# A third buffer of one-hots for an eighth slot of gathered rows, in a graph attention kernel

## The chip, the cores and the metric

The kernel runs on one core of a Trainium2 chip. Its time is the device time of that core in microseconds (us), and the number to watch is the median of several runs. The core has a matrix engine (TensorE, PE in a profile), a vector engine (VectorE, DVE), a scalar engine (ScalarE, ACT), GpSimd (POOL) and SyncE (SP), each with an instruction stream of its own that is worked off in order, and 16 DMA engines that move data between main memory and the core's own memory.

## The reference

One layer of attention on a graph, with 12,500 nodes of 128 features and 212,500 edges that are sorted by their target node (`dst`). Each edge has 128 features of its own. The computation, cut to what matters:

```
Q, K, V = x @ WQ, x @ WK, x @ WV          # per node, 8 heads of 16
Eh      = edge_attr @ WE                  # per edge
score   = exp(clip(sum_per_head(K[src] * Q[dst] / 4 * Eh), -5, 5))
wV, Z   = segment_sum(V[src] * score, dst), segment_sum(score, dst)
h       = x + wV / (Z + 1e-6)
y       = batch_norm(h) * gamma + beta    # mean and variance over all nodes
out     = layer_norm(x + y)               # over the 128 features
```

K and V of the source node are needed for every edge: these rows are fetched by an index. Q of the target node and the sums over the target node are handled with one-hot matrices, because the edges are sorted by target.

## The kernel before, in words

The edges are cut into 1661 tiles of 128. A group has up to 8 tiles in two halves of 4, and there are 208 groups. There are three stages.

**The node table** (loop over `q`, 25 steps). TensorE multiplies the transposed node features by the weights of K and V, VectorE and ScalarE copy the result out of PSUM in turn (L263, L262), and SP stores it as the table `kvd` in main memory (L605). The table is whole only at the end of this stage, so rows of it can be gathered only then. The first 8 groups (0 to 7) do without it. For their edges GpSimd gathers rows of x itself (`slot<-x`), and K and V are made from those: TensorE transposes them (L278, `turn_x`) and multiplies them by the weights (L285, `project`). Some of these groups, `EARLY` of them, are projected during the table's stage at steps spread by `piece` (L614 to L616), and their K and V go into a slot of gathered rows. The others are projected in the main loop one group ahead (`project_main`, L423, called at L681), into other buffers named `t`.

**The main loop** over the groups `g` (L671). The order of all instructions is written by hand: each engine gets its instructions in the order in which these lines call for them. For group g, VectorE multiplies the gathered K by Q times the edge features (`products`, L520), sums per head (L527), clips (L532), and multiplies the gathered V by the exponentials (`message`, L539). Between these it works for other groups; the one that matters here is `onehot(g + 1)`, right behind the message of g, which compares the target numbers of a tile with a row of 0 to 127 (L451 to L454) and so makes the matrix that sums edges into nodes. TensorE uses it one iteration later in `gather_sum` (L554). The one-hots lie in a tile named `oh`.

**The last stage** normalises over the nodes and writes the output. It needs x again, which SP loads into slots that have become free (`load_x`, L407) after the last group has been given one.

**The slots.** `NSLOT` tiles `slot0`, `slot1`, ... of 8 KiB in each partition hold gathered rows. One slot takes two groups of gathered x rows, or one group of K and V rows. A slot becomes free when the message of its group is made (L544), or, for a pair of x groups, when the second of them is projected (L288). Each time `load_kv` (L234) gives the free slot to the next group and queues eight gathers. In the main loop it issues at once all but seven of what is queued. The rest are issued one by one behind steps of VectorE, each with a wait on that step (`pace`, L206), in the order in which the groups come. All gathers are on GpSimd, which works them off in order, so one whose slot is not yet free holds up those behind it. In twelve of the later groups the eighth tile of rows comes by single-row loads on SP instead (`fetch_rows`, L225), into tiles named `byrow`.

Of the kernel before, what the change touches and what calls it, by code (L numbers as in the profile page):

```python
# [8 lines left out]
F32 = mybir.dt.float32  # L9
# [7 lines left out]
P = 128  # L17
# [4 lines left out]
U = 4  # L22
WN = 64
CH = 512
NSLOT = 8
NX = 8
EARLY = 4
RUN = 64
ROWS = 8
FIRST_ROW = 5  # L30
# [32 lines left out]
def gnn_kernel(  # L63
# [35 lines left out]
    wp = lps.enter_context(tc.tile_pool(name="work", bufs=2))  # L99
# [83 lines left out]
    KV, XG, SLOT, PAIR = {}, {}, {}, {}  # L183
    free = list(range(NSLOT))
    pending = list(range(nxg, NG))
# [3 lines left out]
    def slot(i):  # L189
        return rows.tile([P, 2 * G * P], F32, name=f"slot{i}")  # L190
# [15 lines left out]
    def pace(step):  # L206
        if queued:
            f, *a = queued.pop(0)
            tc.add_manual_dep(f(*a).ins, step.ins.name,
                              mybir.DependencyInfo(mybir.DependencyClass.Sync, mybir.DependencyReason.DATA),  # L210
                              reason="pace")
# [34 lines left out]
    for g in range(nxg):  # L246
        if g % 2 == 0:
            PAIR[g // 2] = free.pop(0)
            t = slot(PAIR[g // 2])
# [161 lines left out]
    def nt(g):  # L411
        return sizes[g]
# [29 lines left out]
    def onehot(g):  # L442


        n, m = usizes[2 * g], usizes[2 * g + 1]
        t = wp.tile([P, U * P + U * WN], F32, name="oh", bufs=2)
        one = t[:, :n * P].rearrange("p (a b) -> p a b", b=P)
        two = t[:, U * P:U * P + m * WN].rearrange("p (a b) -> p a b", b=WN)
        OH[g] = [one[:, j, :] for j in range(n)] + [two[:, j, :] for j in range(m)]
        r = rel[:, starts[g]:starts[g] + nt(g)]  # L450
        nc.vector.tensor_tensor(one, iota_ps[:, None, :].to_broadcast([P, n, P]),  # L451
                                r[:, :n, None].to_broadcast([P, n, P]), op=OP.is_equal)
        nc.vector.tensor_scalar(one[:, :, WN], r[:, :n], lim[:, 2 * g:2 * g + 1], None, op0=OP.is_equal)
        pace(nc.vector.tensor_tensor(two, iota_ps[:, None, :WN].to_broadcast([P, m, WN]),  # L454
                                     r[:, n:, None].to_broadcast([P, m, WN]), op=OP.is_equal))
# [156 lines left out]
    NQ = -(-NB // 4)  # L612
    early = min(EARLY, nxg)
    piece = {}  # L614
# [34 lines left out]
    load_kv()  # L649
    ehqe(1)  # L650
    onehot(0)
    within(load, 2)
    turned_onehot(2)
# [17 lines left out]
    for g in range(NG):  # L671
# [26 lines left out]
        if g == NG - 1:  # L698
# [3 lines left out]
            nc.scalar.activation(warm, eps, AF.Sqrt)  # L702
        within(message, g)
        within(onehot, g + 1)
        if g == 2:
            load_last()
# [259 lines left out]
```

## Time and profile before

| what | value |
|---|---|
| median of 3 runs | 2808.24 us (2806.66 to 2818.62) |
| the profiled execution's own time | 2148.92 us |
| its span, from first to last instruction | 2147.0 us |
| busy: TensorE, VectorE, ScalarE, GpSimd | 1681.1, 1640.5, 630.7, 1592.5 us |
| gathers of table rows on GpSimd | 1585, first at 86.2 us, last at 2076.0 us |
| gathers of x rows on GpSimd | 64, first at 3.0 us, last at 82.8 us |
| mean granted TensorE clock | 0.941 |

The profile is of one execution. The times in it are from the start of its span. "Busy" is the time in which an engine executed something. The idle time ahead of a group of instructions is put down to what released the instruction, where that can be seen, and to "issue" where nothing that the profile shows was waited for. The profiled execution is much shorter than the runs. All durations below are from the profiled execution.

### The profile page before, as it was taken

What the parts mean: (1) busy time and instruction counts of PE and PEld (TensorE: products, weight loads), DVE (VectorE), ACT (ScalarE), POOL (GpSimd) and SP (SyncE); (2) the same over time, 40 slices, a digit from 0 to 9 for tenths busy, and PEclk for the clock granted to TensorE, in tenths of its full rate; (3) what the DMA queues carried; (4) which work ended last, traced back from release to release, by engine and by line L of the source; (5) the groups of instructions that cost most, each with busy time, mean ns of one, the idle gap of its engine ahead of it and who ended that gap; (6) DMA issues with size and microseconds to landing.
All of it is one profiled execution on the core that took longest, in us unless ns stands there. A gap on an engine that the chain in (4) does not pass through costs nothing. (4 is left out here: it accounts for less than half of the span.)

```text
span 2147.0 us, 37902 instructions
## 1 busy us (share of the span) xinstructions
PE 1681.1 (78%) x9350; PEld 1094.9 (51%) x9350; DVE 1640.5 (76%) x3571; ACT 630.7 (29%) x2509; POOL 1592.5 (74%) x1681
## 2 busy tenths in 40 slices
PE   8898888877777777777777777777877777777877
PEld 7565555554444444545444545454544544445445
DVE  4669999877877777777787777777777777777766
ACT  3343333222222222232222222222222222222226
POOL 7776777777777777777777777777777777777755
PEclk9999999999999999999999998999899999999988
DMA  9866566555655555656555555555655655655754
GB/s 304 280 190 182 180 203 191 173 180 166 181 168 168 179 167 168 182 168 178 169 173 174 170 180 168 176 171 155 189 173 168 181 167 155 192 171 161 222 163 122
DMA packets 179740, 386.86 MB, mean 180 GB/s; under 512 B 41838, under 2 KB 96151, under 8 KB 179511
## 3 DMA queue, kind: packets, MB, share of 16 engines
q0 software_dynamic: 78128, 212.05, 33.4%
q1 hardware_dynamic: 98038, 169.83, 25.7%
q10 hardware_dynamic: 3345, 2.48, 0.4%
q8 instruction: 77, 1.26, 0.2%
q14 instruction: 152, 1.25, 0.2%
HBM read 364.57 MB, written 19.63 MB: 179 GB/s over the span
## 5 line engine op out<-in xcount | busy, mean ns | idle before, releaser
L199 POOL DMA_INDIRECT slot<-kvd,srcs x1585 | 1502.9, 948 | 490.4 <-issue 202.0
L554 PE MATMUL ps_a<-msg,oh 128*128 128x136 f32 (+1 forms) x3322 | 570.1, 315 | 1.5 <-DVE msg L539 1.5
L520 DVE TENSOR_TENSOR p<-slot,ps_t 128x512 f32<-128x512 f32 (+1 forms) x408 | 272.6, 677 | 356.1 <-DMA slot<-kvd,srcs 328.4
L554 PEld LDWEIGHTS ps_a<-msg,oh 128*128 128x128 f32 (+1 forms) x3322 | 463.5, 183 | 87.5 <-issue 65.3
L534 ACT ACTIVATE ps_m<-s 128x64 f32<-128x64 f32 x208 | 47.3, 227 | 1333.8 <-DVE s L532 1045.7
L490 PE MATMUL ps_e<-ea,w_e 128*128 128x512 f32 x832 | 404.8, 610 | 2.4 <-DMA ea<-eaT 2.1
L576 PE MATMUL ps_m<-ident,at 128*128 128x128 f32 x416 | 101.6, 328 | 320.2 <-DVE oh L454 313.0
L511 PE MATMUL ps_t<-ident,wt 128*128 128x128 f32 x1661 | 243.9, 283 | 92.8 <-DVE wt L503 91.6
L576 PEld LDWEIGHTS ps_m<-ident,at 128*128 128x128 f32 x416 | 66.1, 200 | 412.3 <-ACT q L480 359.5
L503 DVE TENSOR_TENSOR wt<-wt,ps_q 128x512 f32<-128x512 f32 x416 | 265.4, 679 | 1.8 <-PE ps_q L498 1.8
L511 PEld LDWEIGHTS ps_t<-ident,wt 128*128 128x128 f32 x1661 | 184.4, 142 | 135.7 <-DVE wt L503 131.7
L527 DVE TENSOR_REDUCE s<-p 128x64 f32<-128x1024 f32 x208 | 251.6, 1210 | 0.0
L539 DVE TENSOR_TENSOR msg<-slot,ps_m 128x1024 f32<-128x1024 f32 (+1 forms) x204 | 244.7, 1200 | 1.6 <-ACT hx L582 1.4
L492 ACT ACTIVATE wt<-ps_e 128x512 f32<-128x512 f32 x416 | 227.3, 584 | 14.9 <-PE ps_e L490 12.4
L490 PEld LDWEIGHTS ps_e<-ea,w_e 128*128 128x128 f32 x832 | 146.5, 196 | 107.7 <-issue 87.1
L498 PE MATMUL ps_q<-ot,q 64*128 64x512 bf16 x1248 | 171.2, 380 | 0.0
L451 DVE TENSOR_TENSOR oh<-ps_m,rel_i 128x512 f32<-128x512 f32 x208 | 141.8, 682 | 0.0
L498 PEld LDWEIGHTS <-q 64*128 64x128 bf16 x1248 | 44.1, 94 | 186.4 <-issue 161.7
L440 ACT ACTIVATE xw<-hx 128x64 f32 x416 | 84.2, 248 | 59.8 <-issue 52.0
L582 ACT ACTIVATE hx<-ps_m 128x64 f32 x416 | 91.6, 220 | 10.4 <-PE ps_m L577 3.6
L570 DVE SCALAR_TENSOR_TENSOR at<-os,keep,rz 128x128 f32<-128x128 f32 x208 | 73.2, 352 | 24.4 <-DVE rz L566 0.9
L471 PE MATMUL ps_m<-w_q,xw 128*128 128x128 f32 x416 | 88.4, 297 | 1.6 <-ACT xw L440 0.9
(111 smaller groups left out, 1555.3 us busy)
## 6 DMA issues: line engine op xcount, KB each, us to landing
ea<-eaT SPq DMA_DIRECT2D x207, 512.0 KB
rb<-relT SPq DMA_DIRECT2D x414, 64.0 KB
slot<-kvd,srcs POOLq DMA_INDIRECT x1585
byrow<-kvd SPq DMA_DIRECT2D x1536, 1.0 KB
kvd<-t SPq DMA_DIRECT2D x24, 512.0 KB
slot<-xT SPq DMA_DIRECT2D x24, 256.0 KB
out<-o SPq DMA_DIRECT2D x24, 256.0 KB
hx<-xT SPq DMA_DIRECT2D x11, 512.0 KB
```

The costliest lines, as they stand in the source:

```text
L199: return nc.gpsimd.indirect_dma_start(out=out, out_offset=None, in_=table, in_offset=bass.IndirectOffsetOnAxis(ap=srcs[:, e:e + 1], axis=0))
L451: nc.vector.tensor_tensor(one, iota_ps[:, None, :].to_broadcast([P, n, P]), r[:, :n, None].to_broadcast([P, n, P]), op=OP.is_equal)
L490: nc.tensor.matmul(eh, w_e, EA[g][:, a:b, :].rearrange("p a b -> p (a b)"), start=True, stop=True)
L492: nc.scalar.activation(t[:, :(b - a) * P], eh, AF.Copy)
L498: nc.tensor.matmul(QE[g][h], Q3[g][r, k, :], OT[g][r, :(b - a) * P], start=(k == 0), stop=(k == 2))
L503: pace(nc.vector.tensor_tensor(t, t, QE[g][h], op=OP.mult))
L511: nc.tensor.transpose(ps[:, j, :], WT[g][h][:, j * P:(j + 1) * P], ident)
L520: step = nc.vector.tensor_tensor(PR[g][:, c:d, :], KV[g](c, d, 0), PW[g][i][:, c - a:d - a, :], op=OP.mult)
L527: pace(nc.vector.tensor_reduce(SS[g][:, :n, :], PR[g][:, :n, :].rearrange("p t (h d) -> p t h d", d=DH), axis=AX.X, op=OP.add))
L539: nc.vector.tensor_tensor(MSG[g][:, a:b, :P].rearrange("p t (h d) -> p t h d", d=DH), KV[g](a, b, P).rearrange("p t (h d) -> p t h d", d=D ...
L554: nc.tensor.matmul(AGG[g][WN if j >= n else 0:], OH[g][j], MSG[g][:, j, :], start=(j == 0), stop=(j == n - 1))
L576: nc.tensor.matmul(ps, AT[g], ident, start=True, stop=False)
```

## The change

Three constants change. The number of slots goes from eight to seven. The number of groups that are projected beside the node table goes from four to three, so group 3 is projected in the main loop, in iteration 2, like groups 4 to 7 before. The one-hots get a third buffer, of 3 KiB in each partition.

```diff
-NSLOT = 8
+NSLOT = 7
 NX = 8
-EARLY = 4
+EARLY = 3
...
-        t = wp.tile([P, U * P + U * WN], F32, name="oh", bufs=2)
+        t = wp.tile([P, U * P + U * WN], F32, name="oh", bufs=3)
```

Four slots still hold the gathered x of groups 0 to 7 at the start. The steps of the table's stage at which halves of groups are projected move with `EARLY`: they were 3, 5, 8, 10, 13, 16, 18 and 21, and are now 3, 6, 10, 13, 17 and 20. The wait of L451 on TensorE, which kept a one-hot from being written over while the sums of two groups earlier still read it, is no longer in the program. The number of gathers and their order stay. In SP's stream the loads of x for the last stage come one group later, and the last of them comes behind the reading of the flag (L715).

## The prediction

> **What bounds the kernel now.** I read the busy shares first, then the costliest groups, the stretches of time, and last GpSimd's own timeline. The rows of the groups that matter (line, engine, operation, tiles, count | busy, mean ns | idle before, and what ended it):
>
> ```profile
> L199 POOL DMA_INDIRECT slot<-kvd,srcs x1585 | 1502.9, 948 | 490.4 <-issue 202.0
> L520 DVE TENSOR_TENSOR p<-slot,ps_t 128x512 f32<-128x512 f32 (+1 forms) x408 | 272.6, 677 | 356.1 <-DMA slot<-kvd,srcs 328.4
> L451 DVE TENSOR_TENSOR oh<-ps_m,rel_i 128x512 f32<-128x512 f32 x208 | 141.8, 682 | 0.0
> ```
>
> No engine is over 78% busy, so shares do not name the bound; the idle columns do. VectorE waits 328.4 us for gathered rows at L520. GpSimd's 490.4 us before L199 are 1585 gaps of about 0.3 us, which follow every gather whatever its releaser. A gather thus costs 0.95 + 0.30 = 1.25 us, 8 a group 10.0 us. The stretches confirm it (length; PE, PE loads, DVE, ACT, POOL busy; clock; DMA share; GB/s):
>
> ```profile
> 16.00:72.00 56.00, 50.36 (x241) 43.38 (x240) 25.12 (x47) 18.92 (x39) 42.51 (x45) 0.97 1.01 337
> 86.00:170.00 84.00, 75.18 (x424) 49.70 (x425) 60.19 (x134) 35.89 (x111) 60.59 (x64) 0.98 0.65 201
> 170.00:400.00 230.00, 198.93 (x1229) 128.05 (x1227) 219.97 (x484) 80.87 (x324) 172.99 (x183) 1.00 0.63 189
> 400.00:2000.00 1600.00, 1220.69 (x6764) 782.56 (x6765) 1218.07 (x2657) 427.76 (x1760) 1210.89 (x1278) 0.94 0.58 173
> ```
>
> From 400 to 2000 GpSimd issues 1278 gathers in 1600 us, 1.252 us each: it is the bound. From 170 to 400 VectorE is 96% busy and runs at some 7.5 us a group, catching up with rows gathered ahead. In the node table's stage TensorE works 90% of the time and the DMA share is 1.01. A microsecond lost or won by VectorE or TensorE is worth nothing after 400; one lost by GpSimd is worth itself. Its timeline has one place where it stands still in the loop (start, length, [idle before]):
>
> ```profile
> 165.05 0.94 POOL L199 DMA_INDIRECT slot<-kvd,srcs  x1 [0.30 <-DVE oh L454]
> 171.54 0.94 POOL L199 DMA_INDIRECT slot<-kvd,srcs  x1 [5.55 <-DVE msg L539]
> 172.79 0.94 POOL L199 DMA_INDIRECT slot<-kvd,srcs  x1 [0.30 <-DVE oh L454]
> ```
>
> Groups 8 to 15 are 64 gathers, from 86.2 to 166.2; the next, group 16's first, needs a free slot. It starts when the message of group 8 ends, and nothing stops GpSimd again until the last gather at 2076.0. VectorE's timeline gives the messages that free the slots:
>
> ```profile
> 103.88 1.21 DVE L539 TENSOR_TENSOR msg<-slot,ps_m 128x1024 f32<-128x1024 f32 x1
> 116.50 1.21 DVE L539 TENSOR_TENSOR msg<-slot,ps_m 128x1024 f32<-128x1024 f32 x1
> 162.48 1.27 DVE L539 TENSOR_TENSOR msg<-t,ps_m 128x512 f32<-128x512 f32 x2
> 170.06 1.21 DVE L539 TENSOR_TENSOR msg<-slot,ps_m 128x1024 f32<-128x1024 f32 x1
> ```
>
> These are groups 2, 3, 7 and 8. Groups 4 to 7 read "t", not "slot": they free nothing at their message.
>
> **What the Trainium skill says.** "DMA: Bandwidth & Descriptors", section "Anatomy of one DMA — SWDGE (gpsimd) path": DMA engines do not wait on semaphores; the issuing sequencer waits before it dispatches. So a gather without a slot holds every gather behind it, which the 5.55 us at 171.54 show. "Perfetto Trace Analysis", section "Optimization Strategy": a gap that repeats on the engine that should be saturated can mean too few buffers. Here it does not repeat; buffers bind once. "SBUF — State Buffer", section "SBUF: two separate sides": some VectorE operations lock GpSimd out while it writes descriptors. The gathers into slots last 942 to 1097 ns, median 946, so this trace shows no such starving.
>
> **The third one-hot buffer.** L451 rewrites the one-hots of group g-1 when it makes those of g+1, and so waits for TensorE's sums of g-1; with three buffers that wait is gone from L451. The row above gives the idle time ahead of all 208 of them: 0.0. What covers the wait is the message just before, which ends after those sums. Worth 0 us; below zero nothing speaks for a loss, since the same instructions run in the same order.
>
> **Three groups beside the table.** One group's projection leaves the table's stage: on TensorE 8 transposes, which hold it 0.87 us (two runs of four, 0.43 each before the next matmul starts), and 16 matmuls, 4 x 0.865 us from start to start; in all 4.33 us. Also six evacuations of 0.6 to 0.69 us, which lie beside TensorE. TensorE has that stage filled, so the gain for the loop's start is at most 4.33 us. But the DMA share of 1.01 says that the bytes set the pace as much, and none is removed; ACT stood 5.1 us at 51 to 56, waiting for a load, and TensorE 3.06 us behind it. Five halves of groups are projected before that point, and with the change four, so that half's 2.17 us would be waited away there; of the other half's 2.17, saved later, I keep most, since the DMA share is lower after 72. Between 0 and 4.33 I take 1.5 us. GpSimd gains at most some 2.4 us by itself: its 64 gathers of x end at 83.8, and the first of the table begins at 86.2.
>
> **The same projection in the loop.** Group 3 is now projected in iteration 2. Iterations with a projection take 12.6 us (106.20 to 118.81 between first products), the one before without takes 7.5 (98.71 to 106.20). So every message from group 2 on is 5.1 us later, less 1.5: 3.6 us. Its evacuations are all ACT's there, and behind them exp at L534 waits, then the message: that chain is inside the 12.6.
>
> **The seventh slot.** Four slots hold the gathered x of groups 0 to 7 in pairs, three the early groups. With eight, slots 8 and 9 had rows at once (pairs 0 and 1 were projected); with seven only group 8 has. The order of release is then: message 0 for group 9, message 1 for 10, projection 3 for 11, message 2 for 12, projection 5 for 13, projection 7 for 14, message 8 for 15. GpSimd's groups 8 to 13 end at 84.7 + 60 = 144.7. Group 14 needs the transposes of 7, in the trace ending near 149, now 152.6: an early stop, absorbed by what follows. Group 15 needs message 8: 171.54 + 3.6 = 175.1. Group 16 follows 8 x 1.25 = 10.0 later, at 185.1; message 9 is then at 182.8, so nothing stops it further. Before, group 16 began at 171.54. GpSimd is 185.1 - 171.54 = 13.6 us late, with the same 1521 gathers still to come at the same pace, and nothing downstream recovers it: VectorE catches up earlier and waits. Ends: 10.8 (all 4.33 gained) and 15.1 (none).
>
> **Queues and the end.** SP issues the loads of x for the last stage into freed slots, one group later; the last, of 212 columns, now follows message 207 and the reading of the flag. In the trace message 207 starts at 2085.2, that chunk is first used at 2129.3 (the only 212-column sum at L766), and the stores behind it on SP start at 2100.9: cover of some 15 us at the least, cost 0; without it one load, which I estimate at under 5 us, since the issues of four take 1.8. SP's other order, the row loads of the table included, stays. Sum: 0 + 13.6 on the profiled 2148.92 us (span 2147.0 and 1.9 around it) = 2162.5, a ratio of 1.0063.
>
> **Against the median.** The runs' median, 2808.24, is 659 us over that execution, and no view says where. I take the stretch as common to all engines (factor 1.307): 13.6 becomes 17.8, **2826 us**. If it lies outside the loop the time is 2822. A measurement of this kernel can tell about 0.5%, 14 us, from no change.
>
> **Rivals.**
> First, the gather alone is slower in the runs. 659 us over 1649 gathers are 0.40 each, 1.65 instead of 1.25. Then GpSimd is behind from the start (64 of x until 108) and reaches group 15 after 120 gathers, at 5 + 120 x 1.65 = 203, long after message 8 at 175. No stop, before or after; the time stays 2808. It decides from 1.42 us a gather (5 + 120c = 175). For it: a bound of 1.25 a gather gives 2808 most simply if that pace changes. Against: the steadiness of 942 to 1097 ns.
> Second, on the other side: in the runs TensorE is slower against VectorE, and L451 really waits for the sums. The wait lies between the message and the next products, once in each of 208 groups. If it averages w, the third buffer gains 208w against 13.6: it decides from w = 0.065 us, and is a gain of over 0.5% from 0.13. At 0.2 the time is 2808 - 41.6 + 17.8 = 2784. For it: the 170 to 400 stretch, where TensorE is 86% busy and VectorE 96%, so close that little is missing. Against: 0.0 in all 208.
> Third, slots also bind later: the runs' rows land so late that GpSimd stands at a message again, 10 us a time. Two more stops give 2846 us. Against: after 171.54 the trace has none.
>
> **Chances.** The stop at the start as worked out 0.46, gather slower 0.29, one-hot wait 0.18, slots bind later 0.07. The first straddles the 0.5% line a little (2822 is +0.49%), so slower gets 0.48 with the third rival, same 0.33, faster 0.19. The likeliest case's own range is 2819 to 2832. For 8 in 10 I go from 2790, which takes in the unchanged time and half of the gains, to 2838.
>
> **What would show it.** Right: one group fewer gathered before message 8; a stop of GpSimd near 152 and one of 8 to 12 us ended by message 8 near 175; group 16 some 13 us later; the same 1.25 us after; L451 idle 0.0 in both; an iteration 2 of 12.6 us. Wrong: the first table gather over 3 us earlier, idle time ahead of L199 later than 200 us, or VectorE's wait at L520 shrinking by more than GpSimd's stop explains.

## The result, and the profile after

The kernel after took 2854.5 us (median of 22 runs, 2823.55 to 2867.78) against 2812.02 us for the kernel before (22 runs, 2799.83 to 2833.97), a ratio of 1.0125 [1.0101, 1.0149]. The direction of the prediction was right. Its time, 2826 us, was 28.5 us too low, and 2854.5 lies above the range of 2790 to 2838.

The same kernel before takes some 2150 us on some chips (its profile in the prediction is of such an execution) and some 2800 us on others (the runs shown with it, and the result, are of these), so each run below is compared with the kernel before on its own chip. I call them 2150 us chips and 2800 us chips. Only one chip was visited twice, with some 2800 us both times. So it is not shown that the chip itself makes the difference, and not something else at the time.

The rows of the costliest groups that answer to those of before, from the profile of after on a 2800 us chip (line, engine, operation, tiles, count | busy, mean ns | idle before, and what ended it):

```profile
span 2857.9 us, 37907 instructions
...
L199 POOL DMA_INDIRECT slot<-kvd,srcs x1585 | 1499.7, 946 | 1150.1 <-issue 340.0
L490 PE MATMUL ps_e<-ea,w_e 128*128 128x512 f32 x832 | 486.0, 704 | 353.8 <-DMA ea<-eaT 284.4
...
L520 DVE TENSOR_TENSOR p<-slot,ps_t 128x512 f32<-128x512 f32 (+1 forms) x406 | 258.2, 676 | 463.5 <-remote 347.3
...
L461 DVE TENSOR_SCALAR ot<-rb,wiota 128x512 bf16<-128x512 bf16 x207 | 76.0, 367 | 284.5 <-DMA rb<-relT 267.0
...
L576 PE MATMUL ps_m<-ident,at 128*128 128x128 f32 x416 | 111.6, 351 | 120.4 <-DVE oh L454 49.2
...
L451 DVE TENSOR_TENSOR oh<-ps_m,rel_i 128x512 f32<-128x512 f32 x208 | 141.7, 681 | 0.0
```

"Remote" is a wait whose releaser the record does not have. A gather still takes 946 ns, but its idle time is 1150.1 us in place of 490.4. The idle time ahead of L451 is 0.0 here, as predicted, but L461 waits 267.0 us for target rows (`rb`) and L490 284.4 us for edge features (`ea`), both loaded by SP.

This must be laid beside the kernel before on a chip of the same kind, which the prediction did not have. A later run gave that profile:

```profile
span 2788.0 us, 37902 instructions
PE 1930.0 (69%) x9350; PEld 1273.3 (46%) x9350; DVE 1648.7 (59%) x3571; ACT 649.1 (23%) x2509; POOL 1593.5 (57%) x1681
...
L199 POOL DMA_INDIRECT slot<-kvd,srcs x1585 | 1503.5, 949 | 1071.8 <-issue 329.2
...
L490 PE MATMUL ps_e<-ea,w_e 128*128 128x512 f32 x832 | 441.9, 646 | 100.5 <-issue 85.1
L576 PE MATMUL ps_m<-ident,at 128*128 128x128 f32 x416 | 127.0, 398 | 465.5 <-DVE oh L454 361.6
L451 DVE TENSOR_TENSOR oh<-ps_m,rel_i 128x512 f32<-128x512 f32 x208 | 143.0, 688 | 472.9 <-remote 397.6
L520 DVE TENSOR_TENSOR p<-slot,ps_t 128x512 f32<-128x512 f32 (+1 forms) x408 | 260.0, 675 | 168.1 <-remote 129.7
```

Two things stand in it. VectorE, ScalarE and GpSimd are busy nearly as long as on the 2150 us chip (1648.7, 649.1 and 1593.5 us against 1640.5, 630.7 and 1592.5), so on these engines the extra 640 us are waits, not slower work. TensorE is busy 249 us longer (1930.0 against 1681.1 us, at a granted clock of 0.813 against 0.941); how much that adds to the waits of the others was not separated. And L451, for which the prediction read 0.0 us, has 472.9 us of idle time here. The change takes this away, and the waits at L461, L490 and L520 take its place.

The stretches (length; PE, PE loads, DVE, ACT, POOL busy; clock; DMA share; GB/s), first before and then after, both on 2800 us chips:

```profile
170.00:400.00 230.00, 170.37 (x851) 113.29 (x849) 139.67 (x303) 62.77 (x225) 121.67 (x128) 0.83 0.41 123
400.00:2000.00 1600.00, 1095.48 (x5287) 714.29 (x5286) 958.57 (x2088) 348.51 (x1383) 944.97 (x998) 0.81 0.46 135
```

```profile
170.00:400.00 230.00, 173.71 (x878) 112.94 (x877) 139.93 (x306) 64.09 (x229) 114.76 (x122) 0.84 0.42 121
400.00:2000.00 1600.00, 1072.19 (x5144) 668.93 (x5144) 934.66 (x2037) 343.63 (x1351) 921.70 (x974) 0.79 0.45 131
```

In 1600 us GpSimd issues 998 gathers before and 974 after: 1.603 and 1.643 us each. The loss is spread over the whole loop. At the start six gathers are lost (128 to 122), a small part.

### The profile page after: what moved, and what is told of

Its sections match the earlier page's. It is cut to its first block, busy times and chain, and to the rows that moved or that the text cites. A ratio compares the mean times of both kernels' runs of the same rounds, so it can differ in the third digit from the quotient of the medians.

```text
span 2857.9 us, 37907 instructions
## 1 busy us (share of the span) xinstructions
PE 1929.5 (68%) x9350; PEld 1220.7 (43%) x9350; DVE 1645.8 (58%) x3569; ACT 656.5 (23%) x2512; POOL 1589.1 (56%) x1681
## 3 DMA queue, kind: packets, MB, share of 16 engines
q14 instruction: 152, 1.25, 0.1%
## 5 line engine op out<-in xcount | busy, mean ns | idle before, releaser
L199 POOL DMA_INDIRECT slot<-kvd,srcs x1585 | 1499.7, 946 | 1150.1 <-issue 340.0
L490 PE MATMUL ps_e<-ea,w_e 128*128 128x512 f32 x832 | 486.0, 704 | 353.8 <-DMA ea<-eaT 284.4
L554 PE MATMUL ps_a<-msg,oh 128*128 128x136 f32 (+1 forms) x3322 | 643.7, 340 | 37.7 <-issue 35.8
L554 PEld LDWEIGHTS ps_a<-msg,oh 128*128 128x128 f32 (+1 forms) x3322 | 520.0, 201 | 140.5 <-issue 121.3
L520 DVE TENSOR_TENSOR p<-slot,ps_t 128x512 f32<-128x512 f32 (+1 forms) x406 | 258.2, 676 | 463.5 <-remote 347.3
L490 PEld LDWEIGHTS ps_e<-ea,w_e 128*128 128x128 f32 x832 | 166.8, 222 | 491.1 <-issue 460.9
L503 DVE TENSOR_TENSOR wt<-wt,ps_q 128x512 f32<-128x512 f32 x416 | 267.0, 680 | 64.9 <-remote 12.8
L498 PE MATMUL ps_q<-ot,q 64*128 64x512 bf16 x1248 | 209.0, 423 | 62.0 <-issue 61.2
L539 DVE TENSOR_TENSOR msg<-slot,ps_m 128x1024 f32<-128x1024 f32 x203 | 243.5, 1199 | 1.7 <-ACT hx L582 1.5
L471 PE MATMUL ps_m<-w_q,xw 128*128 128x128 f32 x416 | 108.8, 352 | 195.0 <-ACT xw L440 183.9
L461 DVE TENSOR_SCALAR ot<-rb,wiota 128x512 bf16<-128x512 bf16 x207 | 76.0, 367 | 284.5 <-DMA rb<-relT 267.0
L559 ACT ACTIVATE os<-ps_a 128x136 f32<-128x136 f32 x208 | 58.5, 281 | 577.4 <-remote 397.0
L479 DVE SCALAR_TENSOR_TENSOR qr<-ps_m,q 128x128 f32<-128x128 f32 x208 | 58.9, 283 | 197.6 <-ACT hx L582 137.0
L471 PEld LDWEIGHTS ps_m<-w_q,xw 128*128 128x128 f32 x416 | 79.8, 239 | 214.9 <-ACT xw L440 201.0
```

The source lines that it names most:

```text
L199: return nc.gpsimd.indirect_dma_start(out=out, out_offset=None, in_=table, in_offset=bass.IndirectOffsetOnAxis(ap=srcs[:, e:e + 1], axis=0))
L471: nc.tensor.matmul(PQ[g], XW[g], w_q, start=True, stop=True)
L490: nc.tensor.matmul(eh, w_e, EA[g][:, a:b, :].rearrange("p a b -> p (a b)"), start=True, stop=True)
L498: nc.tensor.matmul(QE[g][h], Q3[g][r, k, :], OT[g][r, :(b - a) * P], start=(k == 0), stop=(k == 2))
L503: pace(nc.vector.tensor_tensor(t, t, QE[g][h], op=OP.mult))
L520: step = nc.vector.tensor_tensor(PR[g][:, c:d, :], KV[g](c, d, 0), PW[g][i][:, c - a:d - a, :], op=OP.mult)
```

## Experiments

**Is the result the same on a 2150 us chip, and which part makes it?** The first runs landed on such chips. First the kernel before once more, then the slots and early groups alone (two buffers of one-hots), the early group alone, and a stronger dose of slots:

```diff
 r2_slots7:  -NSLOT = 8  -EARLY = 4     r3_early3:  -EARLY = 4   r4_slots6:  -NSLOT = 8  -EARLY = 4
             +NSLOT = 7  +EARLY = 3                 +EARLY = 3               +NSLOT = 6  +EARLY = 2
```

(With six slots the last chunk of x has a tile of its own.)

> The kernel before, unchanged: what the spread of two equal kernels is, and a profile in the condition of the runs. All theories: a ratio of 1.000, within 0.003. The profile after has 708 of 3074 register steps of SP's single-row loads over 0.4 us where the profile before had none, and many engines standing still together; if that is the condition of the runs and not a part of the change, this profile has a span near 2810 us and such stretches too, some 850 to 900 us of them on SP. If it is a part of the change, the span is near 2150 and there are none.

> Seven slots and three early groups, but two buffers of one-hots. Theory A (slots absorb): GpSimd's lead is one group shorter and in the runs it stands at messages all along; the whole loss is here, a ratio of 1.012 to 1.015. Theory B (the start): the loss is made before 250 us, where one more group is projected in the loop; 1.012 as well. Theory C (the third buffer, by what it does to the order of waits or to where tiles lie): 1.000 to 1.004 here.

> Eight slots and two buffers of one-hots, but three early groups: a slot is free from the start. Theory A: within 1.000 to 1.003, since the lead stays at seven groups. Theory B: 1.010 to 1.013, since the projection in the loop is what costs. Theory C: 1.000 to 1.003.

> Six slots, two early groups, two buffers of one-hots; the last 212 columns of x get a tile of their own. Theory A: every slot less costs about the same or more, 1.025 to 1.035. Theory B: 1.020 to 1.026, all of it before 250 us. Theory C: under 1.008.

Measured: 1.0003 [0.9991, 1.0016], 1.0069 [1.0052, 1.0085], 1.0012 [1.0003, 1.0021] and 1.0123 [1.0106, 1.014], against 2152.54 us. Seven slots cost 14.6 us, six 25.9 us, the early group alone 2.6 us. GpSimd's timeline of the seven-slot kernel (start, length, [idle before]) has the stops that the prediction named, near 152 and near 175:

```profile
148.80 0.94 POOL L199 DMA_INDIRECT slot<-kvd,srcs  x1 [5.96 <-PE ps_t L278]
151.89 0.95 POOL L199 DMA_INDIRECT slot<-kvd,srcs  x1 [2.15 <-issue]
157.03 0.95 POOL L199 DMA_INDIRECT slot<-kvd,srcs  x1 [2.94 <-DVE oh L454]
171.02 0.94 POOL L199 DMA_INDIRECT slot<-kvd,srcs  x1 [8.04 <-DVE msg L539]
```

Then the kernel after itself, the kernel of r2 again, and the same two slot counts without the single-row loads on SP (12 gathers more):

```diff
 r7_norows8 (from before) and r8_norows7 (from after):
-    return [2 * g for g in range(max(FIRST_ROW + span, NX), sizes.count(U) // 2, P // ROWS)]
+    return []
```

> The changed kernel once more, beside the kernel before and beside seven slots with two buffers of one-hots. The same kernel took 2152 us on one chip and 2812 us on another. If this chip is one of the first kind: 1.0063 to 1.0070, as the stop at the start was worked out, and equal to seven slots with two buffers (the third buffer is worth nothing). If it is one of the second kind: 1.012, as measured.

> Seven slots, three early groups, two buffers of one-hots. Theory A (slots absorb stalls): equal to the changed kernel within 0.003 in either kind of condition, so 1.012 where the kernel before takes 2812 us. Theory C (the third buffer loses in that condition): there 1.000 to 1.007, the changed kernel being 0.005 or more above it.

> The kernel before without the single-row loads on SP: the eighth tile of the twelve groups comes by a gather on GpSimd like all others, 12 gathers more, 1536 loads and 3072 register steps on SP fewer. Where the kernel before takes 2152 us: 12 x 1.25 = 15 us more, 1.007. Where it takes 2812 us, if SP's slow register steps (about 890 us of stretches in the profile after) are what holds the others up: far below 1, 0.80 to 0.90. If all the sequencers are slow for a common reason and SP is only one of them: 0.97 to 1.01.

> The changed kernel without the single-row loads on SP. Against the same with eight slots: where the kernel before takes 2152 us, 1.007 over it (the stop at the start). Where it takes 2812 us: if slots absorb SP's stalls, the difference falls to the 1.007 of the start, as these stalls are gone; if it stays at 1.012, the stalls that slots absorb are not SP's.

Measured, against 2151.89 us: after 1.006 [1.0044, 1.0076], seven slots 1.0062 [1.0044, 1.008], no row loads 1.0066 [1.0045, 1.0086], both changes 1.0137 [1.0116, 1.0157]. After and seven slots with two buffers agree: on these chips the third buffer is worth nothing, and the whole change costs 12.3 us. GpSimd's timeline of after there:

```profile
151.26 0.94 POOL L199 DMA_INDIRECT slot<-kvd,srcs  x1 [6.56 <-PE ps_t L278]
...
173.46 0.94 POOL L199 DMA_INDIRECT slot<-kvd,srcs  x1 [8.03 <-DVE msg L539]
...
183.46 0.95 POOL L199 DMA_INDIRECT slot<-kvd,srcs  x1 [0.30 <-DVE p L520]
```

The last line is group 16's first gather, at 183.46. In the kernel before on another chip of that kind it is at 170.01 (profile of r9, below): 13.45 us later, where 13.6 was predicted. Against the 171.54 of the profile that the prediction read it is 11.9 us. Twelve more gathers cost 15.4 us, 1.28 each, so GpSimd's pace is the bound there.

A third set, also on a 2150 us chip, repeats before (one execution, for its profile), r2 and r3, and doubles SP's row loads (24 groups in place of 12, so 12 gathers fewer):

```diff
-ROWS = 8
+ROWS = 16
```

> The kernel before, for its profile on this chip. On a chip of the first kind a span near 2150 us. On one of the second, near 2810: then some 850 to 900 us of slow stretches on SP like the changed kernel's, and GpSimd standing at messages through the whole loop, with eight slots too.

> Seven slots, three early groups, two buffers of one-hots. On a chip of the first kind 1.006 to 1.007, as measured twice. On one of the second: theory A (slots absorb stalls) 1.010 to 1.015; theory C (the third buffer or the layout loses there) 1.000 to 1.006.

> Eight slots, three early groups. On a chip of the first kind 1.001, as measured. On one of the second: theory A 0.998 to 1.003, since the lead is as long as before; theory B (more work in the loop's start) 1.008 to 1.013.

> The kernel before with 16 rows a step by single-row loads instead of 8, so 24 groups instead of 12 get their eighth tile from SP: 12 gathers fewer. On a chip of the first kind GpSimd's 1.25 us a gather gives 15 us less, 0.993, unless SP, with some 3 us more in every iteration, is late with the edge features; then 1.00 or above. On a chip of the second kind SP's slow steps double: 1.05 to 1.3 if SP's steps are what holds the others up, 0.99 to 1.01 if not.

Measured, against 2154.16 us: seven slots 1.0052 [1.0038, 1.0065], early group 1.0012 [1.0003, 1.0021], doubled row loads 1.0272 [1.0253, 1.029]. SP then becomes late even on such a chip. The waits of the last kernel, TensorE's and VectorE's longest (engine, tile, line, what it waited for: us, times, longest):

```profile
PE ps_e L491 <- DMA ea<-eaT: 257.0, 150, 4.1
...
DVE ot L462 <- DMA rb<-relT: 395.7, 176, 4.1
```

These are the two waits that the profile of after shows on a 2800 us chip. So they fit a late SP. In the profile of after on a 2150 us chip the two are 0.9 and 1.2 us.

**Which part costs on a 2800 us chip?** The next set landed on one: seven slots with two buffers again (the kernel of r2), and a kernel with eight slots, three buffers and no row loads.

```diff
 r14_norows8_oh3, beside the edit of r7_norows8:
-        XW[g] = wp.tile([P, P], F32, name="xw", bufs=8)
+        XW[g] = wp.tile([P, P], F32, name="xw", bufs=7)
-        t = wp.tile([P, U * P + U * WN], F32, name="oh", bufs=2)
+        t = wp.tile([P, U * P + U * WN], F32, name="oh", bufs=3)
```

> Seven slots, three early groups, two buffers of one-hots, in search of the condition in which the kernel before takes 2812 us. Where it takes 2152 us: 1.006, as before. Where it takes 2812 us: theory A (the shorter lead loses more there) 1.010 to 1.015; theory C (the third buffer or the layout loses) 1.000 to 1.006.

> Eight slots, four early groups, no single-row loads, seven in place of eight buffers for the copied node columns (room for the third one-hot buffer), and three buffers of one-hots. Where the kernel before takes 2152 us: 1.0066, as without the third buffer; any gain of the buffer would show as less. Where it takes 2812 us: theory C, that the third buffer loses there, gives more than the same without it; SP's slow steps gone, the sign against 1 tells what they cost.

Seven slots with two buffers: 0.9995 [0.9971, 1.0018]. The stop at the start, 12 to 15 us on the other chips, costs nothing here. It is there, 17.77 us ahead of the gather at 182.22, but VectorE reaches the products of group 8 at 229.2 us, and at 232.8 in before. So the 1.25%, though measured on another chip, belongs to the third buffer, or to the room that it takes. The second kernel: 0.963 [0.9586, 0.9674], 2690.31 us, on these chips faster than both kernels by over 100 us. (Seven buffers of `xw` make the room for the third one.)

**A lost wait, the room, or the turn of three?** Two kernels with the room of three buffers in which VectorE waits for the sums of group g-1 again. In the first the three take turns, but one zero is written into the one-hots of g-1 first. In the second only two of the three are used. Beside them the partner of r14 with two buffers, which is the kernel of r7:

```diff
 r15_hold, in onehot(g):                   r17_two_of_three, in onehot(g):
     t = wp.tile(..., name="oh", bufs=3)    +if not OHT:
+    if g - 2 in OHT:                       +    OHT.extend(wp.tile(..., name="oh", bufs=3)
+        nc.vector.memset(                  +               for _ in range(3))
+            OHT[g - 2][0:1, 0:1], 0.0)     +    nc.vector.memset(OHT[2][0:1, 0:1], 0.0)
+    OHT[g] = t                             +t = OHT[g % 2]
```

> The kernel after with one addition: before VectorE makes the one-hots of group g+1 it writes one zero into the first element of those of group g-1, and so waits for TensorE's sums of g-1 as the kernel before does at L451. The room and the places of all tiles stay those of the third buffer. The element is no longer needed, so nothing computed changes. Theory C1 (the freedom of VectorE to go ahead is what costs on chips where the kernel before takes 2800 us): there the ratio to the kernel before returns to 0.998 to 1.004. Theory C2 (the layout or the room costs, not the wait): it stays at 1.010 to 1.015. Where the kernel before takes 2150 us both say 1.005 to 1.008.

> The kernel before without the single-row loads on SP (12 more gathers), two buffers of one-hots: the partner of the run with a third buffer and no single-row loads, which gave 0.963 where the kernel before takes 2800 us. Theory D1 (the third buffer costs through SP, which is the bound there only because of the row loads): 0.958 to 0.968 there. Theory D2 (a third buffer costs whatever SP does): 0.945 to 0.955. D3 (with SP out of the way the wait at L451 is real and a third buffer gains): above 0.97. Where the kernel before takes 2150 us: 1.005 to 1.008, as measured.

> The kernel after, in which the one-hots take the three buffers' room but use only two of them in turn (the third gets one zero at the start), so that VectorE waits at L451 as before. Against the run with seven slots and two buffers only the room and the places of the tiles differ. Theory C2 (the room or the places cost on chips where the kernel before takes 2800 us): there 1.008 to 1.015. Theory C3 (the third buffer costs by its turn, through the order in which VectorE, TensorE, SP and GpSimd meet, and the room is innocent): 0.996 to 1.004 there. Where the kernel before takes 2150 us both say 1.005 to 1.008.

Measured on 2800 us chips: the hold 1.01 [1.0053, 1.0148], two of three 0.9994 [0.997, 1.0019], no row loads with two buffers 0.9693 [0.9653, 0.9732]. Two of three has the room of after by its construction, and the instructions and waits of seven slots with two buffers (plus one write). It and the hold ran on the same chip, in two sets. So the room is innocent, and the turn of three costs. Its groups have before's pattern again:

```profile
L456 DVE TENSOR_TENSOR oh<-ps_m,rel_i 128x512 f32<-128x512 f32 x208 | 143.0, 687 | 485.2 <-remote 404.9
L525 DVE TENSOR_TENSOR p<-slot,ps_t 128x512 f32<-128x512 f32 (+1 forms) x406 | 258.3, 674 | 140.2 <-remote 103.6
```

(L456 and L525 are L451 and L520; the span is 2823.1 us, the median of the runs 2803.65.) The hold was a miss for the simple form of that theory. The wait was in the program, on the write, but VectorE hardly stood there: the profile keeps the pattern of after, with 13.8 us of idle time in all ahead of L456, in six waits (`issue`), and:

```profile
DVE p L525 <- remote: 325.1, 69, 11.6
DVE ot L466 <- DMA rb<-relT: 256.1, 57, 12.3
```

Its 206 writes of 59 ns add at most 12.2 us, 0.4%; its interval reaches down to 1.0053. So a wait on the same sums does not by itself bring the old order back, and what in the turn of three selects the new one stays open.

Without the row loads, three buffers (0.963) are at least as good as two (0.9693); the intervals overlap, on different chips. So in these runs the third buffer's loss needs the row loads beside it. Where the wait goes can be read here, first with two buffers, then with three (L449 and L518 are L451 and L520):

```profile
L518 DVE TENSOR_TENSOR p<-slot,ps_t 128x512 f32<-128x512 f32 (+1 forms) x408 | 265.6, 680 | 299.1 <-remote 225.7
L449 DVE TENSOR_TENSOR oh<-ps_m,rel_i 128x512 f32<-128x512 f32 x208 | 142.7, 686 | 315.2 <-remote 177.1
```

```profile
L518 DVE TENSOR_TENSOR p<-slot,ps_t 128x512 f32<-128x512 f32 (+1 forms) x408 | 266.5, 682 | 594.0 <-remote 274.1
...
L449 DVE TENSOR_TENSOR oh<-ps_m,rel_i 128x512 f32<-128x512 f32 x208 | 142.0, 682 | 0.0
```

315.2 us go ahead of the one-hots, and 294.9 come ahead of the products. The order of the program says why: on TensorE the transposes that the next products need (`turn_back`) stand behind the sums of g-1, so VectorE, let past L451, stands at its next step for the same engine. Only the one-hots themselves get ahead of the wait.

The row loads are not what makes these chips slow, either. Without them the kernel still takes 2715.84 us, 81 us less out of some 640. The 0.80 to 0.90 that were expected if SP's slow steps hold the others up did not come.

**Does the kernel before really stand at L451 there?** One more execution:

> The kernel before, for its profile. Where it takes 2800 us, theory C3 expects VectorE to stand some 400 to 500 us ahead of L451, as with seven slots and two buffers, few waits of TensorE for the edge features at L490 (under 110 us) and of VectorE at L461 for the target rows (under 100 us); if the stop at L451 belongs to seven slots alone, it is near 0 there. Where it takes 2150 us: 0.0 ahead of L451.

It landed on a 2800 us chip. Idle ahead of L451: 472.9 us, as expected (400 to 500); waits for the loads are 14.7 us at L490 and 17.1 us at L461. Its profile is the second one of the section on the result. Its timeline also shows what kind of wait this is (start, length, [idle before]):

```profile
1002.25 0.50 PE L554 MATMUL ps_a<-msg,oh 128*128 128x136 f32 x2
...
1002.77 1.21 DVE L539 TENSOR_TENSOR msg<-slot,ps_m 128x1024 f32<-128x1024 f32 x1
1006.58 0.69 DVE L451 TENSOR_TENSOR oh<-ps_m,rel_i 128x512 f32<-128x512 f32 x1 [2.60 <-PE ps_q L498]
```

The sums of g-1 end at 1002.75 and the message at 1003.98, but L451 starts at 1006.58. VectorE has 111 waits of over 0.3 us at this line, 472.6 us in all, and by the trace (which models the ends of matmuls) the sums had ended before nearly all of that time; VectorE goes on 5.9 us after their end, by the median. So TensorE's work is done, and its release comes late. Of the instructions of TensorE that release others, 31% have the update of their semaphore on record within 0.15 us of their end in this profile, and 99 to 100% in those of before and after on 2150 us chips. (2255 of them have 1981 updates on record here, so some records are missing.)

**Where the loss sits in time.** VectorE's waits of over 0.5 us at L461 in 1000 to 1032 us of after (start, length, [idle before]):

```profile
1001.08 0.35 DVE L461 TENSOR_SCALAR ot<-rb,wiota 128x512 bf16<-128x512 bf16 x1 [0.73 <-issue]
...
1020.89 0.35 DVE L461 TENSOR_SCALAR ot<-rb,wiota 128x512 bf16<-128x512 bf16 x1 [12.20 <-DMA rb<-relT]
1029.05 0.36 DVE L461 TENSOR_SCALAR ot<-rb,wiota 128x512 bf16<-128x512 bf16 x1 [0.56 <-DMA rb<-relT]
```

One iteration takes 19.8 us and the next 8.2. Counted from the start of L451 in iterations 25 to 194, the tenth, fiftieth and ninetieth percentiles of an iteration are 9.0, 13.1 and 16.5 us before, and 8.0, 13.1 and 19.1 after. GpSimd shows the same. From the times of gathers 401 to 1600 of all 1649, with a stop as an idle time of over 1.5 us:

```
kernel on a 2800 us chip       stops   mean us   sum us   gathers from stop to stop
before                          132     3.42      450.9    9.1
seven slots, two buffers        131     3.47      454.4    9.1
two of three                    130     3.65      474.9    9.2
hold                            121     4.05      490.1    9.9
after                           121     4.23      511.3    9.9
```

Stops are fewer and longer, and from before to after they grow by 60.4 us, which is most of the 69.9 us between the two spans (the medians of the result differ by 42.5 us). The stops' sum orders these five profiles as their spans do, 2788.0, 2799.2, 2823.1, 2830.7 and 2857.9.

What SP does in one such stop, in the timeline of after:

```profile
1000.77 15.88 SPq L232 DMA_DIRECT2D byrow<-kvd  x6
1016.67 0.35 SPq L420 DMA_DIRECT2D ea<-eaT  x1
1017.12 1.09 SPq L346 DMA_DIRECT2D rb<-relT  x2
```

Six of this iteration's eight row loads take 15.88 us (all eight of the next one take 3.52), and the loads of `ea` and `rb` stand behind them in SP's order. VectorE's wait for `rb` ends at 1020.89. GpSimd issues its gathers at 1.25 us from 1000.23 to 1012.78, and then stands 9.11 us for the next message. So VectorE waits for SP, SP is slow while GpSimd gathers, and GpSimd then waits for VectorE. That the third buffer lengthens this ring because VectorE may go further ahead, and so releases more gathers at once, fits the numbers (9.9 gathers from stop to stop in place of 9.1); it was argued, not shown.

## Why the prediction was right and wrong

**Right, for the chips whose profile it read.** The shortage of slots was worked out at 13.6 us. On 2150 us chips group 16 is 13.45 us late (11.9 against the profile that was read), after costs 12.3 us (1.006), and seven slots alone 12 to 15 us in three sets. Two more steps hold there: the stop near 152 (6.56 us) and the stop for message 8 (8.03 us, 173.46, predicted 8 to 12 near 175). Iteration 2 was put at 12.6 us; in after it takes 11.8 (96.68 to 108.46 between first products). The Trainium skill's statement in "DMA: Bandwidth & Descriptors", section "Anatomy of one DMA — SWDGE (gpsimd) path", that a wait for a semaphore happens on the issuing sequencer before dispatch, agrees with those stops: no gather starts in their 6.56 and 8.03 us. Two small slips change nothing: the first 64 gathers of table rows end at 165.99 us, not 166.2, and the limits of 0.065 and 0.13 us for the wait at L451 use the 13.6 us of the profile, where the 17.8 us of the runs give 0.086 and 0.153.

**Wrong: "The third one-hot buffer", "Worth 0 us; below zero nothing speaks for a loss, since the same instructions run in the same order."** This step failed. The idle time of 0.0 ahead of L451 held on the profiled chip only. On the chips of the runs VectorE stands 472.9 us ahead of L451, and the third buffer, which takes that wait away, costs about 1.25%: after 1.0125, the same slots with two buffers 0.9995 and 0.9994. "The same instructions in the same order" is true of each engine, but not of where the engines meet: the wait was one of the points where VectorE was held back for TensorE. Why going past it costs time stays open.

**Wrong: "Against the median", the stretch of 1.307 taken as common to all engines.** It carried 13.6 us over to 17.8 us in the runs. The profile of before on a 2800 us chip shows no common stretch: equal busy times and longer waits on VectorE and GpSimd, 15% more busy time on TensorE. The slots' cost there is 0 within 0.3%. Both errors have one root: the sum was made on an execution that was 659 us shorter than the runs, and the waits of the runs were never seen. That the predicted sign was right is luck: the cost named was absent from the runs, and the cost present was put at nothing.

**The rivals.** The first, that the runs gather more slowly and the start costs nothing, was right in its consequence for the slots (0.9995). Its mechanism was wrong: a gather takes 946 to 949 ns as before, only the waits between gathers are longer. It also said that there would be no stop at the start; the profile of before has one of 12.78 us there, ended by a message at 172.92. The second, "L451 really waits for the sums" in the runs, was right that VectorE stands there, at 472.9/208 = 2.3 us each where 0.13 were to be enough for a gain. Its cause was not slower sums: these have ended, and their release is late. Its price was wrong too: 208w would have given over 450 us. It gave no gain, since the next products wait for TensorE as well, but a loss. The third, slots that bind later, was half right. GpSimd does stand at messages after 200 us, which the prediction had named as a sign of being wrong: 26 stops of over 1.5 us in before, 129.4 us in all. But seven slots with two buffers have 28, 133.5 us, and cost nothing more.

## What to carry to other kernels

When the runs and the profiled execution differ by 30%, the profile's zeros are not zeros of the runs: take every wait that it shows as covered to be open, and widen the range for it. Before pricing a wait that a change removes, look at what the same engine does next, and whether that waits for the same thing: here 315.2 us at the one-hots became 294.9 us at the products. A wait's time can also reappear at the next late thing, here SP's loads, and the loop become more uneven and slower. If one engine's queue holds many small loads ahead of the large ones that others need, look there first: dropping them gave 0.963 (with a third buffer) and 0.9693 on 2800 us chips, and 1.0066 on a 2150 us chip.

## What the runs showed of the hardware

The runs fall into two kinds by chip: the medians of before are 2151.89 to 2154.16 us on three chips, and 2796.64 to 2812.02 on others, at granted clocks of 0.941 and 0.813 in two profiles of before. The parts of one change weigh differently on the two kinds: slots 1.0062 against 0.9995, third buffer 0 against 1.25%, row loads a gain of 0.7% against a loss of 3%.

On a 2800 us chip SP's register steps between row loads, 29 and 37 ns by the median, take some 0.7 us each for 708 of 3072 steps in the profile of after (709 in the seven-slot kernel, 673 in before); on a 2150 us chip none of them takes over 0.4 us. They are slow when GpSimd gathers back to back: of the steps with at most two gathers in the 10 us before them 1% or fewer are over 0.4 us in after, with six 17%, with eight 80%. That holds for seven slots and for before too (79% and 80% with eight).

TensorE's releases follow the same pattern. Of those with at most one gather in the 10 us before them none of 29 is late in after (no update on record within 0.15 us of the end), with six 70%, with eight 98%; in the profile of before on a 2150 us chip none of 1687 with eight is. In before on the 2800 us chip 64 of the 111 waits at L451 end 1.5 to 2.3 us after a gather behind which GpSimd stops for over 1.5 us. So what is slow on these chips is not SP alone. Why it happens on one kind of chip is not settled by these runs.
